# Making the C rows of a state-space layer's small product in their other token order by a second TensorE product

## The chip, the cores and the metric

The kernel runs on one core of a Trainium2 chip. The metric is the time of one execution on the device, in microseconds; of the kernel before, three runs are given with their median. The profiles are taken by the hardware profiler from one execution each.

## What is computed

The network has four layers on an input of 4 images, 64 x 64 tokens, 128 channels, each of the form x + layer(group_norm(x)). Only the first concerns us, a selective scan over the tokens in four directions. Cut to what matters (DI = 256 channels, N = 16 states, R = 8, L = 4096 tokens, K = 4 directions):

```python
xs = jnp.stack([x0, x1, x0[..., ::-1], x1[..., ::-1]], axis=1)   # rows, columns, both reversed
x_dbl = jnp.einsum('bkdl,kcd->bkcl', xs, x_proj_weight)          # 8 + 16 + 16 rows
dts, Bm, Cm = jnp.split(x_dbl, [R, R + N], axis=2)
delta = softplus(einsum('bkrl,kdr->bkdl', dts, dt_projs_weight) + dt_projs_bias)
h = exp(delta * A) * h + (delta * u) * B                         # per token, per channel, per state
y = sum over n of h * C
```

The small product in the title is x_dbl: for every block of tokens it gives 8 rows for delta, 16 rows B and 16 rows C.

## The kernel before

Function `layer0` works through 128 units, one for each image b, direction k and chunk c of 512 tokens (`CH`). The 256 channels are two halves s of 128 partitions. A unit has 16 slots, one for each state n. In a slot POOL multiplies du by the broadcast row of B (`dB`, L682), ACT makes two `dA` (L687, one for each half, into three PSUM buffers), and DVE runs two scans (L688) that write the states `h`. Four states make a group g with one `h` tile.

The sum over n with C is a product on TensorE. `h` is transposed, 32 tokens x 4 states at a time (L538, eight transposes a slot into the one PSUM buffer `pt`), ACT copies `pt` to `hT` (L548), and L573 multiplies `hT` by a matrix `W` that holds the C values of 32 tokens in a block-diagonal form; four such products of 32 output rows each stand in one PSUM tile `yT`. This runs 7 slots behind the scans. DVE or ACT then take `yT` into `y` (L589, L587), which SP stores.

The inputs of the next unit are made while the present one runs, by the functions inside `inputs`. A table written out by hand (`TABLE`) says in which slot and at which place of an engine each step is issued; the order on PE, ACT, DVE and POOL is the order of the code. The steps that concern us:

- `project` (slot 6, on PE behind the transposes and products of that slot): the small product L448, two matmuls that add over the halves s, weights `w_x` (48 columns: 8 delta, 16 B, 8 zeros, 16 C), into 48 rows of a PSUM bank. The moving operand is u, for k of 2 and 3 a view of it that runs backwards.
- `rows` (slot 7, on ACT behind the second dA): copies rows 0 to 23 to the SBUF tile `xd` (L451), and SP stores the 16 B rows to memory (L452), from where they come back as `Bb`, broadcast to all partitions (L488, one load for each group).
- `blocks` (slot 7, right behind): copies the 16 C rows to a tile `Ct` in another order of the tokens (L456): token 32 a + t goes to place 16 t + a. SP then stores them in four pieces into the cells of the matrix `W` in memory (L461), which is loaded as `W` once per group (L699).
- `step` (slots 7 and 9, on PE): the product L465 of `xd` (rows 0 to 7, and a row of ones) with `w_dt`, whose other rows are zero, into a PSUM bank; ACT (L468, L471) and DVE (L474) make delta of it. `project` and `step` use one and the same PSUM bank in turn (`spare`).

All these DMAs are issued by SP, one behind the other. In slot 7 the copy hT (L548) follows the copies of `rows` and `blocks` on ACT, and the two dA of slot 8 follow that. Convolutions and products of other images (L161, L179, L371 and others, the "sides") are put into the slots left free, none of theirs on PE into slots 6 to 10 except what had begun.

Of the kernel before, what the change touches and what calls it, by code (L numbers as in the profile page):

```python
# [11 lines left out]
F32 = mybir.dt.float32  # L12
# [72 lines left out]
def layer0(sh, A, x_in, x_out, scr, ahead):  # L85
# [6 lines left out]
    tc, nc = sh.tc, sh.nc  # L92
    with ExitStack() as ctx:
        pool = lambda name, bufs, **kw: ctx.enter_context(tc.tile_pool(name=name, bufs=bufs, **kw))
        wp = pool("l0w", 1)
        tmp = pool("l0tmp", 2)
# [18 lines left out]
        w_x = wp.tile([P, 2, K4, 48], F32, name="w_x")  # L115
# [6 lines left out]
        xd = wp.tile([65, CH], F32, name="xd")  # L122
# [315 lines left out]
        def inputs(k, c, u, par, spare):  # L438

            bd, Wd = scr(f"B{(NCH * k + c) % 3}"), scr(f"W{k // 2}{par}")  # L440
            delta = tmp.tile([P, 2, CH], F32, name="delta")
            du = tmp.tile([P, 2, CH], F32, name="du")
            bank = {}

            def project():
                bank["x"] = spare("xd_ps")[0:48, :]
                for s in range(2):
                    nc.tensor.matmul(bank["x"], lhsT=w_x[:, s, k, :], rhs=u[:, s, :], start=(s == 0), stop=(s == 1))  # L448

            def rows():  # L450
                nc.scalar.copy(xd[0:24, :], bank["x"][0:24, :])  # L451
                nc.sync.dma_start(bd, xd[8:24, :])  # L452

            def blocks():
                Ct = tmp.tile([48, 32, 16], F32, name="Ct", bufs=1)[32:48]
                nc.scalar.copy(Ct, bank["x"][32:48, :].rearrange("n (a t) -> n t a", t=32))  # L456
                for g in range(4):

                    flat = Wd[g, 496 : 496 + 32 * 127 * 16] if k >= 2 else Wd[g]
                    cells = flat.rearrange("(t m a) -> t m a", t=32, a=16)[:, 0:97:32, :].rearrange("t n a -> n t a")  # L460
                    nc.sync.dma_start(cells, Ct[4 * g : 4 * g + 4])  # L461

            def step(s):
                bank[s] = spare("dp")
                nc.tensor.matmul(bank[s], lhsT=w_dt[:, k, s * P : (s + 1) * P], rhs=xd, start=True, stop=True)  # L465

            def grown(s):
                nc.scalar.activation(delta[:, s, :], bank[s], AF.Exp)  # L468

            def logged(s):  # L470
                nc.scalar.activation(delta[:, s, :], delta[:, s, :], AF.Ln, bias=1.0)  # L471

            def limited(s):
                nc.vector.scalar_tensor_tensor(delta[:, s, :], delta[:, s, :], 88.0, bank[s], ALU.min, ALU.max)  # L474

            def weigh():
                nc.gpsimd.tensor_tensor(du, delta, u, ALU.mult)  # L477

            do = dict(x=project, xc=rows, cc=blocks, du=weigh)
            for s in range(2):  # L480
                for name, f in dict(d=step, e=grown, l=logged, m=limited).items():
                    do[f"{name}{s}"] = lambda s=s, f=f: f(s)
            return do, (delta, du), bd, Wd
# [67 lines left out]
        def products(G, q, hT):  # L551
# [64 lines left out]
            x={0, 1, 4, 5, 11, 12, 13, 14, 15},  # L616
            n={0, 1, 2, 3, 4, 11, 12, 14, 15},
# [22 lines left out]
        with tc.manual_schedule(engines=order):  # L640
            idle = lambda: None
            left = opening(any_bank, [idle, fetched, idle, begun, grown_steps, readied])
            u, ready, bd, Wd, Bb = (got[n] for n in ("u", "ready", "bd", "Wd", "Bb"))
            sides.append(Side(rest(left, spare, later), 18 * len(left), 0, 2 * NS * len(left)))
            for i, (b, k, c) in enumerate(units):
# [90 lines left out]
                if i + 1 < len(units):  # L736
                    u, bd, Wd, ready = u_next, bd_next, Wd_next, ready_next
# [1445 lines left out]
```

## Time and profile before

| what | number |
|---|---|
| three runs | 7770.03, 7776.69, 7779.34 us |
| median | 7776.69 us |
| the profiled execution | 7781.59 us, span 7779.7 us |
| busy in the span | PE 81%, DVE 87%, ACT 79%, POOL 73% |
| L448, the small product | 512 records, 251.8 us |
| L451, copy xd | 128, 574 ns at the median |
| L456, copy Ct | 128, 577 ns at the median |

Every f32 matmul shows as two records on PE and two weight loads (PEld), so the 256 matmuls of L448 are 512 records. In a line of the profile come the source line, the engine, the operation, the tiles that are written and read, shapes, count, busy time in us and the mean length of one in ns; behind the next bar, the idle time of the engine ahead of it and who ended it. Lines of instructions of one source line have lengths as minimum, median and maximum in ns. In a timeline the first column is the start in us from the beginning of the span, the second the length. "128*48 128x512" is a matmul of 128 rows in, 48 rows out, with a moving operand of 512 columns.

### The profile page before, as it was taken

What the parts mean: (1) busy time and instruction counts of PE and PEld (TensorE: products, weight loads), DVE (VectorE), ACT (ScalarE), POOL (GpSimd) and SP (SyncE); (2) the same over time, 40 slices, a digit from 0 to 9 for tenths busy, and PEclk for the clock granted to TensorE, in tenths of its full rate; (3) what the DMA queues carried; (4) which work ended last, traced back from release to release, by engine and by line L of the source; (5) the groups of instructions that cost most, each with busy time, mean ns of one, the idle gap of its engine ahead of it and who ended that gap; (6) DMA issues with size and microseconds to landing.
All of it is one profiled execution on the core that took longest, in us unless ns stands there. A gap on an engine that the chain in (4) does not pass through costs nothing. (4 is left out here: it accounts for less than half of the span.)

```text
span 7779.7 us, 141035 instructions
## 1 busy us (share of the span) xinstructions
PE 6337.0 (81%) x52796; PEld 3998.2 (51%) x52796; DVE 6747.1 (87%) x8097; ACT 6112.9 (79%) x9715; POOL 5675.9 (73%) x2590
## 2 busy tenths in 40 slices
PE   7888888878889877888887777787779968687789
PEld 3544444444455444445554444444457756564566
DVE  7999999999999999999999999999966646556678
ACT  7999999989999998999999999999843323314667
POOL 4989999988999998999999999999930023223233
PEclk8999999999999999999999999999999978788899
DMA  6555556545565554555655445455532142231332
GB/s 171 173 163 175 174 173 176 170 169 165 186 183 179 185 177 162 163 177 179 180 184 180 168 156 185 160 188 177 181 107 63 43 128 61 71 108 40 103 95 81
DMA packets 1325855, 1158.87 MB, mean 149 GB/s; under 512 B 694133, under 2 KB 1119697, under 8 KB 1258226
## 3 DMA queue, kind: packets, MB, share of 16 engines
q1 hardware_dynamic: 1323010, 1148.47, 48.0%
q8 instruction: 416, 6.82, 0.4%
q14 instruction: 269, 2.20, 0.1%
q10 hardware_dynamic: 2160, 1.38, 0.1%
HBM read 956.37 MB, written 189.21 MB: 147 GB/s over the span
## 5 line engine op out<-in xcount | busy, mean ns | idle before, releaser
L688 DVE TENSOR_TENSOR_SCAN h<-dA,state,dB 128x512 f32<-128x512 f32 x4096 | 4921.0, 1266 | 204.4 <-POOL dB L682 79.5
L682 POOL TENSOR_TENSOR dB<-du,Bb 128x1024 f32<-128x1024 f32 x2048 | 4811.7, 2385 | 342.9 <-DVE h L688 208.6
L538 PE MATMUL pt<-ident,h 128*128 128x128 f32 x16384 | 2221.0, 279 | 875.7 <-ACT hT L548 860.0
L687 ACT ACTIVATE dA<-delta,A_neg 128x512 f32<-128x512 f32 x4096 | 2761.1, 697 | 157.6 <-DVE h L688 129.7
L538 PEld LDWEIGHTS pt<-ident,h 128*128 128x128 f32 x16384 | 1807.0, 142 | 1926.3 <-ACT hT L548 1704.7
L548 ACT COPY hT<-pt 128x1024 f32<-128x1024 f32 x2048 | 2080.2, 1016 | 164.7 <-PE pt L538 146.4
L573 PE MATMUL yT<-hT,W 128*32 128x256 f32 x16384 | 1379.6, 409 | 0.4
L573 PEld LDWEIGHTS yT<-hT,W 128*32 128x32 f32 x16384 | 456.0, 150 | 342.5 <-issue 330.9
L161 PE MATMUL cv<-xn,taps 128*128 128x512 f32 x936 | 527.0, 644 | 2.8 <-DVE delta L474 2.8
L1155 POOL TENSOR_TENSOR xg<-xg,so 128x1024 f32<-128x1024 f32 x16 | 39.3, 2466 | 636.5 <-PE pu L1155 613.6
L1900 POOL TENSOR_TENSOR S<-S,sm 128x784 f32<-128x784 f32 x128 | 191.1, 1493 | 419.1 <-DVE sm L1898 256.3
L477 POOL TENSOR_TENSOR du<-delta,u 128x1024 f32<-128x1024 f32 x128 | 304.3, 2377 | 79.0 <-DVE delta L474 78.9
L465 PE MATMUL dp<-xd,w_dt 65*128 65x512 f32 x512 | 288.8, 646 | 69.9 <-ACT Ct L456 47.0
L448 PE MATMUL xd_ps<-u,w_x 128*48 128x512 f32 x512 | 251.8, 615 | 23.6 <-DVE e L360 18.1
L1907 ACT ACTIVATE S<-S,mx 128x196 f32<-128x196 f32 x512 | 227.8, 448 | 35.9 <-DVE mx L1934 35.4
L161 PEld LDWEIGHTS cv<-xn,taps 128*128 128x128 f32 x936 | 139.2, 188 | 180.5 <-issue 160.4
L914 ACT ACTIVATE h<-pf,b 128x512 f32<-128x512 f32 x128 | 87.7, 687 | 117.2 <-PE pf L913 99.2
L474 DVE SCALAR_TENSOR_TENSOR delta<-delta,dp 128x512 f32<-128x512 f32 x256 | 170.6, 667 | 4.3 <-ACT delta L471 1.0
L1862 PE MATMUL pt<-ident,S 128*98 128x128 f32 x1024 | 166.3, 287 | 3.5 <-POOL S L1900 2.0
L465 PEld LDWEIGHTS dp<-xd,w_dt 65*128 65x128 f32 x512 | 76.5, 188 | 174.5 <-ACT Ct L456 99.9
L1155 POOL TENSOR_TENSOR WX<-wr,Xs 128x544 f32<-128x544 f32 x40 | 58.0, 1449 | 148.2 <-issue 61.8
L471 ACT ACTIVATE delta<-delta 128x512 f32<-128x512 f32 x256 | 165.9, 649 | 0.0
(378 smaller groups left out, 7030.6 us busy)
## 6 DMA issues: line engine op xcount, KB each, us to landing
Bb<-l_B SPq DMA_DIRECT2D x512, 1024.0 KB
W<-l_W SPq DMA_DIRECT2D x512, 256.0 KB
l_y<-y SPq DMA_DIRECT2D x127, 512.0 KB
u<-l_xr SPq DMA_DIRECT2D x64, 512.0 KB
u<-l_xw SPq DMA_DIRECT2D x64, 512.0 KB
y<-l_y SPq DMA_DIRECT2D x56, 512.0 KB
V<-l_v SPq DMA_DIRECT2D x512, 49.0 KB
y<-l_y SPq DMA_DIRECT2D x80, 256.0 KB
```

Of the source, the lines that this page charges most:

```text
L161: nc.tensor.matmul(pm, lhsT=taps[:, s, t, :], rhs=xn[:, dy : dy + 8, dx : dx + 64], start=(t == 0), stop=(t == 8),)
L448: nc.tensor.matmul(bank["x"], lhsT=w_x[:, s, k, :], rhs=u[:, s, :], start=(s == 0), stop=(s == 1))
L465: nc.tensor.matmul(bank[s], lhsT=w_dt[:, k, s * P : (s + 1) * P], rhs=xd, start=True, stop=True)
L477: nc.gpsimd.tensor_tensor(du, delta, u, ALU.mult)
L538: nc.tensor.transpose(pt[:, j, s, :], G["h"][:, s, t0 : t0 + 32, :].rearrange("p t n -> p (t n)"), sh.ident)
L548: return lambda: nc.scalar.copy(hT, pt.rearrange("p j s d -> p j (s d)"))
L573: nc.tensor.matmul(U["yT"][e][32 * jo : 32 * jo + 32, qo % 2, :], lhsT=U["Ws"][G["g"]][:, :, 4 * q + j], rhs=hT[:, j, :], start=((e, jo) n ...
L682: nc.gpsimd.tensor_tensor(dB, du, B_now[:, q : q + 1, :].to_broadcast([P, 2, CH]), ALU.mult)
L687: nc.scalar.activation(dA, delta[:, s, :], AF.Exp, scale=A_neg[:, k, s, n : n + 1])
L688: nc.vector.tensor_tensor_scan(h[:, s, :, q], dA, dB[:, s, :], state[:, s, n : n + 1], ALU.mult, ALU.add)
L1900: nc.gpsimd.tensor_tensor(Sv, Sv, U["sm"].unsqueeze(2).to_broadcast([P, 4, 196]), ALU.mult)
L1907: nc.scalar.activation(Sn, Sn, AF.Exp, bias=U["mx"][:, n : n + 1], accum_out=sm[:, n : n + 1])
```

## The change

The small product is made as two products for each half s. One has the first 32 weight columns and takes u as it stands; it writes rows 0 to 31 of the bank. The other has the 16 C columns and takes u in the order that `blocks` needs, so that its neighbouring columns are 32 tokens apart in SBUF; it writes rows 32 to 47. ACT then copies all 48 rows to `xd` in one instruction, the copy to `Ct` and its tile are gone, and the four stores of the cells read rows 32 to 47 of `xd`. `step` is as before; the rows of `w_dt` that meet the C rows are zero.

```diff
             def project():
                 bank["x"] = spare("xd_ps")[0:48, :]
+                blocked = lambda v: v.rearrange("p (a t) -> p t a", t=32)
                 for s in range(2):
-                    nc.tensor.matmul(bank["x"], lhsT=w_x[:, s, k, :], rhs=u[:, s, :], start=(s == 0), stop=(s == 1))
+                    for rows, v in ((slice(0, 32), u[:, s, :]), (slice(32, 48), blocked(u[:, s, :]))):
+                        nc.tensor.matmul(
+                            bank["x"][rows, :],
+                            lhsT=w_x[:, s, k, rows],
+                            rhs=v,
+                            start=(s == 0),
+                            stop=(s == 1),
+                            skip_group_check=True,
+                        )
 
             def rows():
-                nc.scalar.copy(xd[0:24, :], bank["x"][0:24, :])
+                nc.scalar.copy(xd[0:48, :], bank["x"])
                 nc.sync.dma_start(bd, xd[8:24, :])
 
             def blocks():
-                Ct = tmp.tile([48, 32, 16], F32, name="Ct", bufs=1)[32:48]
-                nc.scalar.copy(Ct, bank["x"][32:48, :].rearrange("n (a t) -> n t a", t=32))
+                Ct = xd[32:48, :].rearrange("n (t a) -> n t a", a=16)
                 for g in range(4):
```

## The prediction

> **What bounds the kernel now.** I read the page's groups first, then a window inside the first layer, then the timeline of one unit, then the waits of the lines that the change touches. The first layer runs from about 70 to 5660 us of the span; its loop has 128 units of 16 slots, and the change touches every unit once. The two costliest groups of the page:
>
> ```profile
> L688 DVE TENSOR_TENSOR_SCAN h<-dA,state,dB 128x512 f32<-128x512 f32 x4096 | 4921.0, 1266 | 204.4 <-POOL dB L682 79.5
> L682 POOL TENSOR_TENSOR dB<-du,Bb 128x1024 f32<-128x1024 f32 x2048 | 4811.7, 2385 | 342.9 <-DVE h L688 208.6
> ```
>
> A slot has two scans (about 1.2 us from start to start) and one dB of 2.38 us: DVE and POOL run at one pace. The window 900 to 1000 us shows all engines busy (columns: length, then busy time of PE, PEld, DVE, ACT, POOL):
>
> ```profile
> 900.00:1000.00 100.00, 86.08 (x648) 48.69 (x646) 96.90 (x89) 94.65 (x137) 93.46 (x42) 1.00 0.63 190
> ```
>
> DVE is the bound, with ACT close behind: it feeds DVE the dA of every scan. PE looks slack, but one pt buffer makes PE and ACT take turns: transposes, hT copy, transposes. So time added on PE between two hT copies reaches DVE, if ACT must wait for it. The change does so in slots 6 and 7. One typical unit (start, length in us):
>
> ```profile
> 2025.10 0.67 PE L573 MATMUL yT<-hT,W 128*32 128x256 f32 x8
> ...
> 2025.81 1.92 PE L448 MATMUL xd_ps<-u,w_x 128*48 128x512 f32 x4
> ...
> 2027.66 1.09 PE L538 MATMUL pt<-ident,h 128*128 128x128 f32 x8
> ...
> 2028.34 0.58 ACT L451 COPY xd<-xd_ps 24x512 f32<-24x512 f32 x1
> ...
> 2028.95 0.58 ACT L456 COPY Ct<-xd_ps 16x512 f32<-16x512 f32 x1
> 2028.95 4.26 SPq L452 DMA_DIRECT2D l_B<-xd  x1
> 2029.55 1.01 ACT L548 COPY hT<-pt 128x1024 f32<-128x1024 f32 x1
> ...
> 2029.58 1.12 PE L465 MATMUL dp<-xd,w_dt 65*128 65x512 f32 x2 [0.23 <-ACT Ct L456]
> ...
> 2030.46 0.69 ACT L687 ACTIVATE dA<-delta,A_neg 128x512 f32<-128x512 f32 x1
> ...
> 2031.24 2.46 DVE L688 TENSOR_TENSOR_SCAN h<-dA,state,dB 128x512 f32<-128x512 f32 x2 [0.20 <-issue]
> ```
>
> To be seen: the product L448 ends at 2027.73, the copies xd and Ct and then hT stand in one row on ACT, the next dA follows hT, and the scan at 2031.24 starts 0.09 us after that dA ended, with DVE idle for 0.20.
>
> **Removed.** The copy Ct: 0.58 us of ACT per unit, 74 us in all. Also the wait of dp (L465) for it. ACT's idle time is no measure of the gain; DVE's is. What DVE waits for over the whole run:
>
> ```profile
>   POOL dB L682: 79.5, 43
>   ACT dA L687: 70.9, 90
>   issue: 35.1, 45
> ```
>
> In 67 of 126 units the slot-8 scan starts on its dA with no slack; cut at 0.58 each, DVE's idle time ahead of those scans sums to 25 us. That is all that the removed copy can give. Copying 48 rows in place of 24 costs nothing: 24 rows take 574 ns and 16 take 577. That L456 reads PSUM in steps of 128 bytes costs nothing either, by the same two numbers.
>
> **Moved.** The five DMAs of the step stay the same, all on SP in the same order: the store of B, then four stores of C cells. All now wait for one copy. In 74 of the 126 units the cells start some 0.2 us earlier (they waited for Ct behind an issue of 0.34 us). In the other 52 the issue of the B store itself takes over 4 us, as here (4.26), and nothing is won. Queued behind them on SP is the load of Bb for the last group, for which POOL's dB of slot 12 waits. The whole copy comes later if the product does, so this is no gain of its own.
>
> **Added.** Each of the two products per unit becomes two, of 32 and of 16 rows. A product shows as two records, so 4 records become 8, all of 512 columns. A record now takes (1.92 - 0.592) / 3 = 0.44 us from start to start. Two things decide the price.
>
> *Do they run side by side?* The eight L573 records above go to four blocks of 32 output rows; each lasts 0.41 us on average, and all eight lie within 0.67 us. So blocks of 32 rows overlap. The change's two blocks (rows 0 to 31, 32 to 47) are of this kind: I take it that they overlap. If they don't, four records come on top, 1.72 us at the present rate.
>
> *How fast is the second one read?* Its moving operand takes u in steps of 32 elements, 128 bytes. No row has that. The reversed reading of u for k of 2 and 3 is no slower (592 ns at least and at the median), but it steps by 4 bytes. The nearest rows, where SBUF is stepped through:
>
> ```profile
> L1950 PEld LDWEIGHTS po<-PT,V x4096: 106/110/178, 7265.1 to 7772.7; 98*32 98x32 f32 x196
> ```
> ```profile
> L573 PEld LDWEIGHTS yT<-hT,W x16384: 131/150/183, 141.1 to 5731.8; 128*32 128x32 f32 x200
> ```
> ```profile
> L371 ACT COPY xw<-e x52: 1116/1136/1156, 178.6 to 4187.8; 128x512 f32<-128x512 f32 x52
> ```
> ```profile
> L471 ACT ACTIVATE delta<-delta x256: 619/647/683, 84.3 to 5655.5; 128x512 f32<-128x512 f32 x128
> ```
>
> PE loads 32 weights a row in 110 ns from neighbouring elements and in 150 ns in steps of 64 bytes: 1.25 ns more per element (0.8 by the minima). ACT writes 512 elements in steps of 32 bytes in 1136 ns against 647: 0.96 ns more per element. The ends are thus 0.43 us per record (steps cost nothing) and 0.43 + 512 x 1.25 ns = 1.07 us. I take ACT's 0.96, which lies between the two readings of the weight load: 0.43 + 0.49 = 0.92 us. The weight load is the nearer engine, but its extra is spread over only 32 elements.
>
> The Trainium skill speaks against this change here: its page "SBUF — State Buffer", in the section "Door 1: The DMA port swizzle", says that SBUF has lines of 16 bytes, that two or more accesses per line are needed for full bandwidth, and that fp32 can be stepped freely only within four elements. It gives no price; if one access per line meant half the rate, an estimate from that page would be 0.86 us per record, and the 121 us below would be 97. The L573 weight load and the L371 copy agree with it; the moving operand itself no row here shows.
>
> **The sum.** With 0.92 us the 16-row records take 4 x 0.92 and the product ends 4 x (0.92 - 0.43) = 1.96 us later. In the unit shown: the product ends at 2029.69, the transposes at 2028.75 + 1.96 = 2030.71, hT starts 0.09 later at 2030.80 in place of 2029.55 (the new copy, from 2029.73 to 2030.31, is done by then). dA and scan follow hT: 1.25 us late. dp waits for products queued behind the transposes, 1.7 us late; e (L468) then comes 1.3 us late, and delays the second dA by about the same. Nothing behind makes this up on DVE, since ACT is idle for only 0.13 us per unit in slots 8 to 11 together, on average.
>
> I worked the other units in the same way from their rows. In 67 the slot-8 scan has no slack behind its dA: they lose 1.31 us each, 88 us. In 26 the slack is about 0.44: 0.97 each, 25 us. In 30 it is about 1.2, because DVE waits there for dB or has other work: 0.27 each, 8 us. The last 3 lose nothing. Together 121 us. Given back: in the 52 units where the B store's issue is what holds SP, the late Bb load need not come later still, and DVE's 0.46 us of waits for POOL in the slots after, 24 us in all, may cover some of the delay. I count half: 110 us. The profiled execution took 7781.6 us (span 7779.7), 4.9 above the median of the runs shown; its sum is 7892, and from the median 7776.7 it is **7887 us**. By 0.8 and 1.25 ns per element the product ends 1.64 and 2.56 us later, worth 89 and 184 us by the same units; less the 24 at the low end, this case spans 7842 to 7961.
>
> **The rivals.**
> 1. *Steps are free (faster).* Both blocks run side by side at 0.43 us, the product ends when it does now, and ACT is rid of 0.58 us ahead of hT. For it: the strided PSUM read and the reversed read cost nothing, and PE takes an f32 element only every 0.83 ns. Against it: the stepped weight load, on PE itself. Price: minus 25 us, 7752. The point from which it decides: worked through the same units, the gain is gone once the product ends more than about 0.6 us later, that is at 0.58 us per 16-row record.
> 2. *They don't overlap, steps free.* Plus 1.72 us per product, 97 us by the same units: 7874. This lies within the forecast's span though its cause is another; a partial price (0.6 to 1.6 us) gives 0 to 89.
> 3. *The new product does neither:* no overlap and stepped reading, 4 x 0.92 = 3.68 us later. Only the slack is hidden: some 2.5 us per unit, 320 us, 8097. Against it are the L573 rows.
>
> **How the numbers follow.** Forecast 62 in 100; rival 2 and partial prices 8; rival 1, 18; rival 3, 8; something dearer 4. To leave out no more than 2 in 10 the range must take in rival 1 beside the forecast: 7745 to 7965, which leaves out rival 3 and the dear tail. A measurement of this kernel tells about 0.2%, 15.6 us, from no change. Faster by more: most of rival 1, 14. Within: the rest of it and small partial prices, 7. Slower: 79.
>
> **What would show it.** In the profile after: L448's 16-row records start beside the 32-row ones (overlap) or behind them; they follow one another at 0.92 us (steps cost) or 0.43. ACT's xd copy waits for PE in most units, where the product now ends 0.6 us ahead of it at the median; DVE's 70.9 us of waits for dA grows to some 170 or more. If the records are at 0.43 and overlap, my sum is wrong at its first term, and the kernel is faster. If the records are slow but the time hardly moves, the slack in slots 7 and 8 was misjudged.

## The result: slower by 1.6%

The changed kernel takes 7906.15 us (median of 4 runs, 7892.95 to 7913.51), the kernel before 7776.57 in the same series: a ratio of 1.0163, interval 1.0151 to 1.0176, or 130 us. The forecast was 7887, slower. The profiled execution took 7909.98 us, its span is 7907.0.

The page of the changed kernel, with the scan, the small product (now L450) and the one copy (L460):

```profile
L696 DVE TENSOR_TENSOR_SCAN h<-dA,state,dB 128x512 f32<-128x512 f32 x4096 | 4924.1, 1267 | 267.0 <-ACT dA L695 103.6
...
L450 PE MATMUL xd_ps<-u,w_x 128*32 128x512 f32 (+1 forms) x1024 | 465.9, 822 | 23.5 <-DVE e L360 18.1
...
L460 ACT COPY xd<-xd_ps 48x512 f32<-48x512 f32 x128 | 75.1, 587 | 147.3 <-PE xd_ps L450 142.2
```

The scans are as long as before; DVE's idle time ahead of them has grown from 204.4 to 267.0 us, and the wait that leads is now the one for dA. The product keeps PE busy for 465.9 us in place of 251.8. ACT now idles 142 us ahead of its copy, for the product. The groups of L450, with the two shapes kept apart (busy, mean ns | idle before):

```profile
L450 PE MATMUL xd_ps<-u,w_x 128*16 128x512 f32 x512 | 465.3, 1041 | 0.0
L450 PE MATMUL xd_ps<-u,w_x 128*32 128x512 f32 x512 | 245.7, 603 | 23.5 <-DVE e L360 18.1 <-DVE xr L425 4.3
```

245.7 and 465.3 sum to 711, but the line as a whole is busy for 465.9: the 32-row records lie inside the time of the 16-row ones. The blocks overlap, and the stepped ones set the length. The same unit as in the prediction, in the changed kernel's timeline:

```profile
2074.80 0.67 PE L581 MATMUL yT<-hT,W 128*32 128x256 f32 x8
...
2075.51 3.64 PE L450 MATMUL xd_ps<-u,w_x 128*32 128x512 f32 x8
...
2079.08 1.09 PE L546 MATMUL pt<-ident,h 128*128 128x128 f32 x8
2079.18 0.59 ACT L460 COPY xd<-xd_ps 48x512 f32<-48x512 f32 x1 [1.05 <-PE xd_ps L450]
...
2080.26 1.01 ACT L556 COPY hT<-pt 128x1024 f32<-128x1024 f32 x1 [0.49 <-PE pt L546]
2080.70 1.12 PE L473 MATMUL dp<-xd,w_dt 65*128 65x512 f32 x2
2080.84 0.69 DVE L597 TENSOR_TENSOR y<-y,yT 128x512 f32<-128x512 f32 x1 [0.67 <-PE yT L581]
2081.17 0.70 ACT L695 ACTIVATE dA<-delta,A_neg 128x512 f32<-128x512 f32 x1
...
2081.92 0.60 ACT L476 ACTIVATE delta<-dp 128x512 f32<-128x512 f32 x1
2081.96 2.46 DVE L696 TENSOR_TENSOR_SCAN h<-dA,state,dB 128x512 f32<-128x512 f32 x2 [0.43 <-ACT dA L695]
```

The product lasts 3.64 us in place of 1.92. From its start to the slot-8 scan it is now 6.45 us (2081.96 - 2075.51), before it was 5.43 (2031.24 - 2025.81): 1.02 us lost in this unit. ACT stands idle twice, 1.05 us for the product and 0.49 for the transposes behind it, and saves 0.58 from the missing copy.

From the first scan to the last, the two profiled executions differ by 119.2 us (5604.7 and 5723.8). Their spans differ by 127.3: 1.9 more stand ahead of the first scan and 6.2 behind the last one. The stretch behind the last scan, where nothing was changed, takes 2053 to 2068 us in the profiles of all the kernels here, so what follows counts the loop where a profile is compared.

### The profile page after: what moved, and what is told of

Its sections match the earlier page's. It is cut to its first block, busy times and chain, and to the rows that moved or that the text cites. A ratio compares the mean times of both kernels' runs of the same rounds, so it can differ in the third digit from the quotient of the medians.

```text
span 7907.0 us, 141677 instructions
## 1 busy us (share of the span) xinstructions
PE 6525.8 (83%) x53308; PEld 4019.2 (51%) x53308; DVE 6763.0 (86%) x8097; ACT 6051.9 (77%) x9587; POOL 5678.3 (72%) x2590
## 5 line engine op out<-in xcount | busy, mean ns | idle before, releaser
L696 DVE TENSOR_TENSOR_SCAN h<-dA,state,dB 128x512 f32<-128x512 f32 x4096 | 4924.1, 1267 | 267.0 <-ACT dA L695 103.6
L450 PE MATMUL xd_ps<-u,w_x 128*32 128x512 f32 (+1 forms) x1024 | 465.9, 822 | 23.5 <-DVE e L360 18.1
L450 PEld LDWEIGHTS xd_ps<-u,w_x 128*16 128x16 f32 (+1 forms) x1024 | 69.3, 108 | 236.5 <-issue 177.5
L460 ACT COPY xd<-xd_ps 48x512 f32<-48x512 f32 x128 | 75.1, 587 | 147.3 <-PE xd_ps L450 142.2
L482 DVE SCALAR_TENSOR_TENSOR delta<-delta,dp 128x512 f32<-128x512 f32 x256 | 171.8, 671 | 12.4 <-ACT delta L479 10.4
```

The costliest lines, as they stand in the source:

```text
L450: nc.tensor.matmul(bank["x"][rows, :], lhsT=w_x[:, s, k, rows], rhs=v, start=(s == 0), stop=(s == 1), skip_group_check=True,)
L696: nc.vector.tensor_tensor_scan(h[:, s, :, q], dA, dB[:, s, :], state[:, s, n : n + 1], ALU.mult, ALU.add)
```

## The experiments

The theory: the stepped read doubles the time of the 16-row records; the product ends 1.7 us later, ACT's copies follow it, and DVE waits for dA. The rivals: the split itself costs, the single copy costs, or the stepped read disturbs other engines.

**The read, plain.**

```diff
-                blocked = lambda v: v.rearrange("p (a t) -> p t a", t=32)
+                blocked = lambda v: v
```

> The changed kernel, but the 16-row product takes u as it stands, element after element; the C rows then stand in the wrong order of tokens, so this leaves the reordering out. Theory (the stepped read of u doubles the time of the 16-row records, 0.86 us in place of 0.43, and the late end of the product delays ACT and then DVE): all records at 0.43 us, the product within 2.0 us, and only the gain of the removed copy is left: 25 us below the kernel before, some 7752 (7735 to 7765). Rival A (the cost is the split: more weight loads and records that do not overlap): as slow as the changed kernel, 7906. Rival B (the cost is the one copy of 48 rows, for which all five stores now wait, or the next copy waiting for stores that read xd): 7906 too.

Measured: 7754.73 us, ratio 0.9972 (0.9961 to 0.9984). The product lasts 1.89 us at the median. Its 16-row group, to be set beside the 1041 ns of the changed kernel:

```profile
L450 PE MATMUL xd_ps<-u,w_x 128*16 128x512 f32 x512 | 246.1, 604 | 0.0
```

This is the theory's number, and rivals A and B fall: the split and the one copy are both in this kernel. The stepping of one operand turns 22 us of gain into 130 of loss.

**The split alone, in the kernel before.**

```diff
-                    nc.tensor.matmul(bank["x"], lhsT=w_x[:, s, k, :], rhs=u[:, s, :], ...)
+                    for rows in (slice(0, 32), slice(32, 48)):
+                        nc.tensor.matmul(bank["x"][rows, :], lhsT=w_x[:, s, k, rows], rhs=u[:, s, :], ...)
```

> The kernel before with nothing changed but the split: two products of 32 and 16 rows per half, both reading u as it stands, then the two copies as before (xd, and Ct in the other order out of PSUM). Theory: the blocks overlap, so the product ends no later than 2.0 us after its start; 7777, within 10 us. Rival A (the split costs): 7870 or more, with the 16-row records starting only when the 32-row ones are over. Rival B: 7777, as the theory.

Measured: 7778.17 us, ratio 1.0004 (0.9995 to 1.0014): no change. The two blocks together keep PE busy for 244.9 us, where the one product took 251.8. Twice the records cost nothing where they overlap, and the gain of the experiment before comes from the copy that went, not from the split.

**The delay without the steps.**

```diff
-                for s in range(2):
+                for s in (0, 1, 0, 1):
```
(and the plain read)

> The changed kernel with the plain read of the first experiment (C rows in the wrong order), and the four products of a unit are made twice, the second time over the first. That makes the product end 1.72 us later with no stepped read at all. Theory: it is the late end of the product that costs, whatever makes it late, so the time is that of the changed kernel, 7906 within 15 us. Rival (the stepped read also disturbs other readers of SBUF, such as the scans on DVE or the copies on ACT): clearly below 7906, 7850 or so, as the late end alone was worth 97 us by the units' rows.

Measured: 7913.98 us, ratio 1.0179 (1.0164 to 1.0194), against 1.0163 of the changed kernel: the same within the intervals. The product lasts 3.60 us here and 3.64 there. Who waits for L450, in this kernel and then in the changed one (us, times):

```profile
  ACT xd L460: 150.0, 109
```
```profile
  ACT xd L460: 142.2, 107
```

In the kernel before this wait was 14.8 us in 22 times. The late end explains the loss to within the some 15 us that the two intervals leave; if the stepped read disturbs others, it is by less than that.

**Half of the delay.**

```diff
-                for s in range(2):
+                for s in (0, 0, 1):
```
(and the plain read)

> The changed kernel with the plain read (C rows in the wrong order), and the product of the first half s made twice, the second time over the first: the product ends 0.86 us later than with the plain read, half of what the stepped read makes it. Theory (the late end costs only what exceeds the slack in front of the copies and of the scan): from the prediction's units 16 us above the kernel before, 7793; with the shortfall that the full delay showed, up to 7810. Rival (no slack: every part of a us costs alike, so half the delay costs half of the 155 us between the plain and the stepped read): 7832.

Measured: 7824.09 us, ratio 1.0060 (1.0043 to 1.0077), 45 us above the kernel before in its series. That misses the theory's 7793 (16 above); its upper 7810 (33 above) lies at the lower end of the interval, the rival's 7832 (55 above) inside it. In the profile the loop is 36 us longer than before, where the units' first scans account for 21 and the steps behind them for the rest. From plain read over half to full delay, each against the kernel before in its own series, the time goes -22, +45, +137 us: the first half costs 67 and the second 92. The intervals alone do not settle that difference; the profiled loops say the same, 62 and 85. So there is some slack, but little. A straight line between the first two meets the kernel before at a delay of some 0.3 us, not at the prediction's 0.6.

**How the steps are priced.** Three kernels with other steps, otherwise the changed kernel:

```diff
-                blocked = lambda v: v.rearrange("p (a t) -> p t a", t=32)
+                blocked = lambda v: v.rearrange("p (a t) -> p t a", t=2)            # 8 bytes
+                blocked = lambda v: v.rearrange("p (a t) -> p t a", t=4)            # 16 bytes
+                blocked = lambda v: v.rearrange("p (a h l) -> p h a l", h=16, l=2)  # pairs
```

> The changed kernel with u read in steps of 2 elements (8 bytes, two accesses per 16-byte line); the C rows then stand in another order, so this is for the price of the read alone. If a line of 16 bytes is what counts: records at 0.43 us and about 7755. If any step at all costs: 0.86 us and about 7906.

> The same with steps of 4 elements (16 bytes, one access per line); the C rows in another order again. If a line of 16 bytes is what counts: 0.86 us per record and about 7906, as with 128 bytes. If it is the distance (or the same bank again and again at 128 bytes): between 0.43 and 0.86 us.

> The same with pairs: two neighbouring elements, then a step of 128 bytes, so that every line that is touched is read twice but the distance is that of the change; the C rows in another order again. If accesses per line are what counts: 0.43 us per record and about 7755. If the long steps themselves cost, half of the dear price: about 0.64 us per record, and some 30 to 50 us above the plain read.

Measured: 7755.95, 7918.83 and 7747.74 us, one run each. The 16-row groups of the three kernels, in this order:

```profile
L450 PE MATMUL xd_ps<-u,w_x 128*16 128x512 f32 x512 | 260.9, 631 | 0.0
```
```profile
L450 PE MATMUL xd_ps<-u,w_x 128*16 128x512 f32 x512 | 489.9, 1091 | 0.0
```
```profile
L450 PE MATMUL xd_ps<-u,w_x 128*16 128x512 f32 x512 | 250.9, 611 | 0.0
```

A record lasts 631 ns in steps of 8 bytes, 1091 in steps of 16, 611 with pairs 128 bytes apart; plain it lasts 604, in the changed kernel 1041. A record begins before the last one has ended, so the rate is seen from start to start inside a product: by the medians 0.46, 0.91 and 0.445 us in the three, 0.43 plain, 0.86 in the changed kernel. Not the distance counts, but how many of the neighbouring elements are used: two within 16 bytes go at nearly full speed, one at half or a little less. This is the rule of the Trainium skill's page "SBUF — State Buffer" (section "Door 1: The DMA port swizzle"), now seen on the moving operand.

**The steps on the write side.**

```diff
-                            bank["x"][rows, :],
+                            o,    # for the 16 rows: .rearrange("n (t a) -> n a t", a=16)
...
-                            rhs=v,
+                            rhs=u[:, s, :].rearrange("p (a t) -> p a t", t=32) if rows.start else u[:, s, :],
```

> The changed kernel with the same order of the C rows, but the steps on the other side of TensorE: the 16-row product reads u as it stands and writes its columns into PSUM in steps of 16 elements (64 bytes). One copy of 48 rows, nothing left out. Theory (the price is the stepped read of SBUF, one element per 16-byte line): the records go at 0.43 us and the time is that of the plain read, 7755 (7745 to 7765), below the kernel before. Rival (TensorE's write to PSUM is as dear in steps as its read of SBUF): records at 0.86 us and 7906; a dearer write than that, above 7906.

Measured: 7751.27 us, ratio 0.9971 (0.9961 to 0.9981). This version makes the same C rows in the same order with the one copy, and it beats both kernels. Its 16-row group, and who waited for the product:

```profile
L452 PE MATMUL xd_ps<-u,w_x 128*16 128x512 f32 x512 | 247.5, 607 | 0.0
```
```profile
  PE xd_ps L452: 11.3, 5
```

TensorE writes PSUM in steps of 64 bytes as fast as in a row (607 ns against 604). The same section of that page says that any access to PSUM that is not contiguous slows matmuls significantly; these writes were not slowed, and the measurement decides for this form.

**The reordering copy, later.**

```diff
-            (7, "act1"): ("xc", "cc"),
+            (7, "act1"): ("xc",),
+            (13, "act2"): ("cc",),
...
-                nc.scalar.copy(Ct, bank["x"][32:48, :].rearrange("n (a t) -> n t a", t=32))
+                nc.scalar.copy(Ct, xd[32:48, :].rearrange("n (a t) -> n t a", t=32))
```

> Not a part of the change but what the diagnosis points to: one product of 48 rows as before, one plain copy of all 48 rows to xd in slot 7, and the reordering copy to Ct made out of xd in slot 13, where ACT waits for DVE, with the four stores of the cells behind it. Theory: slot 7 has 0.58 us less on ACT and the product ends as before, worth 25 us; the four stores no longer stand ahead of the Bb load on SP (1.66 us), worth up to another 24; the copy in slot 13 costs nothing as long as ACT's idle time there (0.2 to 0.3 us a slot, over slots 13 to 3) takes it: 7752, 7725 to 7765. Rival (ACT's idle time in slots 13 to 15 is no slack, since POOL and DVE stand close there): the copy of 0.6 to 1.1 us comes back on DVE, 7780 to 7850.

Measured: 7853.61 us, ratio 1.0103 (1.0088 to 1.0118): the rival was right, and the time lies even a little above its 7850. The copy, and DVE's waits ahead of the scans in this kernel:

```profile
L456 ACT COPY Ct<-xd x128: 1094/1136/1160, 72.1 to 5733.5; 16x512 f32<-16x512 f32 x128
```
```profile
  ACT dA L688: 123.5, 177
```

Out of SBUF the reordering copy takes 1136 ns, out of PSUM it took 577. In the trace slot 13 grows from 2.46 to 3.08 us on average, so more than half of the copy comes back on DVE in that one slot; DVE's waits for dA went from 70.9 to 123.5 us. The likely reason, not tested alone: ACT's idle time of 0.2 to 0.3 us per slot is where it waits for its turn, not a store of time that a long instruction can draw on as a whole.

## Why the prediction was right, and which terms were not

- *The blocks overlap*: right, by the trace of the change and by the split alone.
- *The read is slow in steps*: right, and this decided between the forecast and rival 1 (free steps). The size was too high: 0.92 us per record was forecast, (3.64 - 1.04) / 3 = 0.87 was measured, close to the 0.86 of half the rate. The product ends 1.72 us later, not 1.96. Read from the prediction's units that was worth 97 us in place of 121.
- *The removed copy gives 25 us*: right, 22 with the plain read and 23 with the steps on the write side.
- *The units' sum*: the step that failed is that the shift of slot 8's first scan was taken as the loss of the whole unit. Measured per unit, from slot 6 on, in the three groups of the prediction (the last two of its four taken together; 125 units, without the first and the last):

| units | at the first scan of slot 8 | at the first scan of slot 9 | at slot 6 of the next unit |
|---|---|---|---|
| 67 without slack | 1.17 us | 1.24 | 1.22 |
| 26 with some 0.44 | 0.61 | 0.91 | 0.98 |
| 32 with more | 0.26 | 0.29 | 0.40 |
| sum | 102 us | 116 | 120 |

  The first scans alone make 102 us, near the 97 of the table at this delay. The second scan of slot 8 shifts no more than the first (1.17, 0.62 and 0.26 us, together 103 us), so the second dA added nothing, as the prediction had it. The next instruction on DVE is the one that was left out: L482 (L474 before), which in slot 9 takes the delta that ACT makes from dp by L476 and L479. dp stands on PE behind transposes and products that are themselves late. In the 26 units with slack at the first dA, that delta comes 1.09 us later, and DVE had only 0.34 us to spare for it in the kernel before. What L474 waited for in the kernel before, and L482 in the changed one (us, times):

```profile
  ACT delta L471: 1.0, 2
```
```profile
  ACT delta L479: 10.4, 55
```

  Counted up to the first scan of slot 9, this wait and the like bring 14 us, and the rest of the unit 4.
- *The give-back of 12 us*: wrong, there was none. In the 52 units the issue of the B store did shorten, from 4.4 to 3.1 us on average, and the Bb load started no later (0.05 us earlier). But POOL's dB of slot 12 started 1.13 us later all the same, since with three dB buffers it waits for scans that are late (it starts 0.13 us behind the second scan of slot 9 at the median, before and after).
- So that 110 came near 119 was in part luck: a price that was 24 us too high met 18 us of shifts that were left out, 12 us of relief that did not come, and first scans that cost 5 us more than the table's 97.
- *The signs*: the xd copy waits in 107 units in place of 22, as forecast; DVE's waits for dA grew to 103.6 us, well short of the 170 named. A part of the delay shows under other names: 100.4 us for dB in place of 79.5, and 35 us of the y sums (L597) for the products, where it was 3.8.

## What to carry to other kernels

Reordering inside a matmul is not free on its moving side: an f32 operand that used one element of every 16 or 128 bytes was read at half speed or a little less here, and pairs were enough to avoid it. The same reordering on the output side cost nothing here, so put the steps where the result is written. Before a product is made longer on a slack-looking engine, look who stands behind it in that slot: here ACT and PE take turns over one PSUM buffer, and about two thirds of the delay went through to DVE, by more than one path. From the plain read to the doubled plain product the loop grew by 146.8 us, some 1.17 us per unit for a product that ends 1.72 us later.

## What the hardware showed besides

- A stepped read of 16 bytes was a little slower than one of 128: 0.91 us against 0.86 from record to record. Why is open.
- Steps of 8 bytes cost 8% from record to record (0.46 against 0.43 us), pairs 128 bytes apart 4% (0.445).
- ACT reads SBUF in steps of 128 bytes at 1136 ns for 512 elements, PSUM in the same steps at 577.
- Two blocks of 32 and 16 output rows overlap even when one takes twice as long as the other: 465.9 us busy together, 465.3 for the slower alone.
